# Attention and feed-forward block on one core: the projections of q, k, V and the output issued as four matmuls of 32 outputs each

## The chip, the cores and the metric

The kernel runs on one core of one Trainium2 chip. The metric is the device time of one execution in microseconds (us). Names of engines: PE is TensorE's matmul, PEld its weight load, ACT is ScalarE, DVE is VectorE, POOL is GpSimd, SP is SyncE. PSUM is the memory that matmuls write to, SBUF the one that everything else works in.

## What is computed

One transformer block on x of 4 batches x 1024 tokens x 256 features, all in float32:

```python
# attention, 16 heads of 16
xn = layernorm(x)
q, k, v = split(xn @ Wqkv.T)                 # 256 features each, 16 heads of 16
attn = softmax(q @ k.T / sqrt(16))           # per batch and head, 1024 x 1024
y = concat_heads(attn @ v) @ Wout.T
x = x + layernorm(y)
# feed-forward, 256 -> 1024 -> 1024 -> 1024 -> 256
xn = layernorm(x)
h = silu((xn @ w1.T) * s1) * ((xn @ w2.T) * s2)
h = gelu((h @ h1.T) * sh1)
h = gelu((h @ h2.T) * sh2)
x = x + layernorm((h @ w3.T) * s3)
```

## The kernel before

`tile_fast` does the work. (`tile_general` is a slower path for other inputs; it runs only when a flag says so, and the change doesn't touch it.) A first stage computes the attention of all four batches, a second one the feed-forward network of all tokens.

**The units of attention.** The 16 heads are taken in four groups of four. A unit is one batch, one group of heads and one half (512) of the queries: 4 x 4 x 2 = 32 units, each with 16 tiles. A tile is 128 keys x 512 queries for two heads. Its scores (`exponentials`, L451) are two matmuls that use 64 of the 128 rows of the array each and all 128 columns, side by side; ACT then takes the exponential of both in one instruction of 128 x 1024 (L452). Two tiles together hold the four heads of a group. The weighted sums (`weigh`, L459) are for each pair of tiles four matmuls, one for each head, which use all 128 rows and 32 columns of the array each and write to partitions 0 to 31, 32 to 63, 64 to 95 and 96 to 127 of one PSUM tile. A float32 matmul becomes two weight loads and two matmuls on the chip, so one call of `weigh` is eight matmul instructions in two rounds of four. A matmul of the float32r kind (scores, feed-forward) becomes one of each.

**The main loop** (L868 to L888) goes round five or six times for each unit. Once round makes the scores of three tiles (`TURN`; fewer where a step has borrowed a PSUM tile), weighs the tiles made the time before, two at a time, and then calls `side.take()`.

**The side steps.** `Side` holds lists of steps, and `take` runs those that are due, at most one of them with matmuls ("tensor" steps). So in PE's program order one such step stands between the weighted sums of one round and the scores of the next. These steps are the prologue of the next batch (layer norm, transposes of x, projections), and the end of each unit and each batch (division, transposes, output projection). Three of them are what the change touches:

- `project(w, m, h)` in `prologue`, L324: q (w = 0) or k (w = 1), 128 of the 256 features, 512 tokens. Two matmuls (over `c`, the halves of the 256 inputs) with 128 x 128 weights from `wqk_sb`, that read 128 x 512 of `xT`. 8 steps for each batch, 32 in all.
- `values(t0)` in `prologue`, L315: V of 256 tokens. Four matmuls whose weights are 128 x 128 of `xT`, that read 128 x 256 of `wv_sb`. 4 steps for each batch.
- `project(t0)` in `ending`, L516: the output projection of 256 tokens. Four matmuls whose weights are 128 x 128 of `oT`, that read 128 x 256 of `wo_sb`. 4 steps for each batch.

Each of these steps writes one PSUM tile from `ps_misc`, which has a single buffer; DVE copies it out (ACT in the first and the last steps). The first batch's projections for the first groups of heads run ahead of the loop (L836 to L849). The last half's output projection runs inside the feed-forward stage, whose matmuls (L697, L750) have 128 x 128 weights.

The transposes (L305, L478, L480, L506) are matmuls of 128 x 128 by an identity.

Of the kernel before, what the change touches and what calls it, by code (L numbers as in the profile page):

```python
# [18 lines left out]
P = 128  # L19
HEADS = 16  # L20
DH = 16
SLOT = 32
# [13 lines left out]
NQ = 512  # L36
# [4 lines left out]
@with_exitstack  # L41
def tile_attention_ffn_block(ctx: ExitStack, tc: tile.TileContext, x, wqk, wv, wo, w1, w1s, w2, w2s, h1, h1s, h2, h2s, w3, w3s, out):

    nc = tc.nc
    B, S, D = x.shape
    bad = ctx.enter_context(tc.tile_pool(name="flag", bufs=1)).tile([1, 1], I32, name="bad")
    tile_fast(tc, x, wqk, wv, wo, w1, w1s, w2, w2s, h1, h1s, h2, h2s, w3, w3s, out, bad)
    failed = nc.values_load(bad[0:1, 0:1], min_val=0, max_val=1 << 24)
    with tc.If(failed > 0):
        tile_general(tc, x, wqk, wv, wo, w1, w1s, w2, w2s, h1, h1s, h2, h2s, w3, w3s, out)
# [46 lines left out]
def tile_fast(ctx: ExitStack, tc: tile.TileContext, x, wqk, wv, wo, w1, w1s, w2, w2s, h1, h1s, h2, h2s, w3, w3s, out, bad):  # L115
    nc = tc.nc
    B, S, D = x.shape
    HID = w1.shape[1]
    DC = D // P
# [3 lines left out]
    HPT = P // DH  # L123
# [53 lines left out]
    with ExitStack() as actx, ExitStack() as rctx:  # L177
        aw = actx.enter_context(tc.tile_pool(name="aw", bufs=1, side="right"))

        wqk_sb = aw.tile([P, DC, 2, HEADS, DH], F32, name="wqk_sb")  # L180
        wv_sb = aw.tile([P, DC, D], F32, name="wv_sb")
        wo_sb = aw.tile([P, DC, D], F32, name="wo_sb")
# [51 lines left out]
        def misc(name):  # L234
            return ps_misc.tile([P, NQ], F32, tag="misc", name=name)

        def check_weights(n, c):
# [15 lines left out]
            def count(j):  # L253
                def run():
                    w, r = (t[:, NQ * j : NQ * (j + 1)] for t in (st["w"], st["r"]))
                    i = k * (WIDE // NQ) + j
                    nc.vector.scalar_tensor_tensor(w, w, 1.0, r.bitcast(F32), ALU.mult, ALU.not_equal, accum_out=misses[:, i : i + 1])
                    if NQ * (j + 1) == WIDE:
                        nc.gpsimd.dma_start(out=rows(rounded[n]).bitcast(F32), in_=st["r"].bitcast(F32).rearrange("p (i d) -> p i d", i=rows_at_once[n]))

                return run

            return [Step(load, 0, False), Step(cast, 3, False)] + [Step(count(j), 1, False) for j in range(WIDE // NQ)]

        def to_scalar(o, i, scale=1.0):
            nc.scalar.activation(o, i, AF.Copy, scale=scale)  # L266

# [3 lines left out]
        def prologue(b, space, copy):  # L271

            st = {}
# [36 lines left out]
            def values(t0):  # L310
                def run():
                    pv = space(f"pv_{b}_{t0}").rearrange("p (t d) -> p t d", d=D)
                    for i in range(2):
                        for c in range(DC):
                            nc.tensor.matmul(pv[:, i, :], st["xT"][:, c, (t0 + i) * P : (t0 + i + 1) * P], wv_sb[:, c, :], start=c == 0, stop=c == DC - 1)  # L315
                    copy(cv[:, t0 : t0 + 2, :], pv)

                return run

            def project(w, m, h):  # L320
                def run():
                    pp = space(f"p{w}_{b}_{m}_{h}")
                    for c in range(DC):
                        nc.tensor.matmul(pp, wqk_sb[:, c, w, HPT * m : HPT * (m + 1), :], st["xT"][:, c, h * NQ : (h + 1) * NQ], start=c == 0, stop=c == DC - 1)  # L324
                    hi, lo = (cq[w, m, k][:, h * NQ : (h + 1) * NQ] for k in ("hi", "lo"))
                    scale = 1.0 if w else 1.0 / math.sqrt(DH)
                    copy(hi, pp, scale)
                    nc.vector.scalar_tensor_tensor(lo, pp, scale, hi.bitcast(F32), ALU.mult, ALU.subtract)

                return run  # L330
# [11 lines left out]
            def total(m):  # L342
                def run():
                    if m == 0:
                        st["norm"] = work.tile([P, NT], F32, tag="norm", name=f"norm_{b}", bufs=1)
                        st["sum"] = work.tile([P, DC], F32, tag="sum", name="sum", bufs=1)
                        st["sum2"] = work.tile([P, DC], BF16, tag="sum2", name="sum2", bufs=1)
                    t = st["sum"][:, m : m + 1]
                    nc.vector.tensor_reduce(t, cq[1, m, "hi"].bitcast(F32), AX.X, ALU.add)
                    nc.gpsimd.tensor_tensor(st["sum2"][:, m : m + 1], t, t, ALU.mult)  # L350

                return run
# [46 lines left out]
            flags = [Step(total(m), 1, False) for m in range(DC)]  # L399
# [95 lines left out]
        def ending(b, h, copy):  # L495

            st = {}

            def transposes(c):
                def run():  # L500
                    if c == 0:
                        st["oT"] = work.tile([P, DC, NQ], F32, tag="oT", name=f"oT_{b}_{h}", bufs=1)
                        st["y"] = (both if h else work).tile([P, TPQ, D], F32, tag="y", name=f"y_{b}_{h}", bufs=1)
                    pt = misc(f"po_{b}_{h}_{c}")
                    for t in range(TPQ):
                        nc.tensor.transpose(pt[:, t * P : (t + 1) * P], on[h][:, t, c * P : (c + 1) * P], ident)  # L506
                    copy(st["oT"][:, c, :], pt)

                return run

            def project(t0):
                def run():
                    py = misc(f"py_{b}_{h}_{t0}").rearrange("p (t d) -> p t d", d=D)
                    for i in range(2):
                        for c in range(DC):
                            nc.tensor.matmul(py[:, i, :], st["oT"][:, c, (t0 + i) * P : (t0 + i + 1) * P], wo_sb[:, c, :], start=c == 0, stop=c == DC - 1)  # L516
                    copy(st["y"][:, t0 : t0 + 2, :], py)

                return run

            def gather(i):
                def run():
                    st["mv"] = norms.gather([st["y"][:, j, :] for j in range(i, i + 2)], i, st.get("mv"))

                return run

            def root():
                st["ln"] = norms.root(st["mv"])

            def apply(i0):  # L530
                def run():
                    for i in range(i0, i0 + 2):
                        norms.apply(st["y"][:, i, :], st["y"][:, i, :], st["ln"], i)

                return run

            def residual(i):
                def run():
                    xr = xs[b][:, h * TPQ + i : h * TPQ + i + 2, :]
                    nc.vector.tensor_add(xr, xr, st["y"][:, i : i + 2, :])  # L540

                return run

            return (
                [Step(transposes(c), 1) for c in range(DC)] + [Step(project(t), 1) for t in range(0, TPQ, 2)]
                + ([Step(open_ffn, 0, False)] if (b, h) == (B - 1, NH - 1) else [])
                + [Step(gather(i), 1, False) for i in range(0, TPQ, 2)] + [Step(root, 0, False)]
                + [Step(apply(i), 1, False) for i in range(0, TPQ, 2)] + [Step(residual(i), 1, False) for i in range(0, TPQ, 2)]
            )
# [253 lines left out]
        def feed_forward():  # L803

            chain = ends[B - 1, NH - 1]
            for n in range(len(halves_of)):

                gated(ffn["a"], 2 if n else 1)
                if n + 1 < len(halves_of):
                    chain[0].extend(prepare(n + 1, to_scalar))  # L810
                if n == 1:
                    side.add(judge())
                gelu_layer(ffn["b"], ffn["a"], "h1")
                gelu_layer(ffn["a"], ffn["b"], "h2")
                side.flush()
                chain = side.add(finish(n, ffn["a"]), True)
            side.flush()
# [10 lines left out]
        norm, xt, qk, v, flags = prologue(0, first_space, first_copy)  # L828
# [39 lines left out]
        while weighed < len(tiles):  # L868
# [7 lines left out]
            while weighed + 2 <= n:  # L876
                b, g, h, c, _ = tiles[weighed]
# [252 lines left out]
```

## Time and profile before

| | us |
|---|---|
| median of 3 runs (1335.29 to 1335.87) | 1335.56 |
| the profiled execution, its own time | 1335.65 |
| its span, first to last instruction | 1333.7 |
| PE busy | 1271.8 (95%) |
| PEld busy | 797.1 (60%) |
| DVE busy | 724.3 (54%) |
| ACT busy | 696.6 (52%) |
| POOL busy | 120.7 (9%) |

The span is the stretch of one profiled execution from its first to its last instruction; 1.95 us of the execution's own time lie around it. The granted clock of PE is 0.994 of full speed over the span. Attention takes the first 680 us or so and the feed-forward stage the rest.

A row of the timeline merges neighbouring instructions of one line: start in us, length in us, engine, line, operation, output<-inputs, array shape (rows*columns), operand, count, and in brackets the idle time before it with what ended it. The recorded end of a matmul is modelled and lies after the start of the next one, so the distance from start to start is what a matmul takes from PE; I read lengths of work that way.

### The profile page before, as it was taken

The numbers are of one execution on the slowest core, as the hardware profiler recorded it, in microseconds if no ns is written. First come the engines' busy times: TensorE is split into PE (matmuls) and PEld (weight loads), VectorE is DVE, ScalarE is ACT, GpSimd is POOL, SyncE is SP. The second block draws the span as 40 slices with busy tenths as digits, with TensorE's granted clock in tenths as the row PEclk, the third lists the DMA queues.
The fourth block names the chain that finished last, engine by engine and source line by source line (L and its number), as shares of the span: only waits on it lengthen the run. The fifth ranks groups of instructions, "written<-read, shape, count | busy, mean of one in ns | idle before, by whom it ended". The sixth has DMA issues, their size and how long they took to land.

```text
span 1333.7 us, 18779 instructions
## 1 busy us (share of the span) xinstructions
PE 1271.8 (95%) x7042; PEld 797.1 (60%) x7042; DVE 724.3 (54%) x1561; ACT 696.6 (52%) x847; POOL 120.7 (9%) x166
## 2 busy tenths in 40 slices
PE   7999999999999999989999999999999999999996
PEld 3334333343343434333478888888888888888885
DVE  3575669756696455645482553735436364362623
ACT  4587788877887787888741321414224141231410
POOL 6120112111111000000000000000000000000000
PEclk9999999999999999999999999999999999999998
DMA  4675344544444433235220000000000000000000
GB/s 133 152 194 111 98 97 113 122 111 99 120 106 106 77 64 62 45 64 179 79 111 1 1 16 1 17 0 0 16 1 16 0 16 2 0 17 0 17 0 19
DMA packets 38661, 79.61 MB, mean 60 GB/s; under 512 B 11296, under 2 KB 21152, under 8 KB 38560
## 3 DMA queue, kind: packets, MB, share of 16 engines
q1 hardware_dynamic: 30672, 53.66, 18.3%
q0 software_dynamic: 7360, 24.12, 5.5%
q8 instruction: 58, 0.95, 0.3%
q10 hardware_dynamic: 528, 0.52, 0.1%
q14 instruction: 43, 0.35, 0.1%
HBM read 28.98 MB, written 15.73 MB: 34 GB/s over the span
## 4 chain that ended last, share of the span: by engine, by line
PE 78%; DVE 9%; ACT 7%; issue 2%; POOL 1%; DMA 0%; SPq 0%; ACTq 0%; POOLq 0%; DVEq 0%
PE ph L697 35%; PE acc L459 13%; PE s L451 8%; ACT e L452 6%; PE pg L697 6%; PE pz L750 4%; PE p L324 4%; PE py L516 2%; PE pv L315 2%; DVE top L468 2%; PE po L480 1%; DVE o L269 1%; DVE sg L713 1%; DVE st L93 1%; DVE ha_lo L702 1%
## 5 line engine op out<-in xcount | busy, mean ns | idle before, releaser
L452 ACT ACTIVATE e<-s 128x1024 f32<-128x1024 f32 x512 | 486.3, 1036 | 131.1 <-PE s L451 117.8
L459 PE MATMUL acc<-e,vaug 128*32 128x512 f32 x2048 | 256.5, 603 | 2.9 <-POOL vaug L429 2.9
L733 ACT ACTIVATE a<-ph,h_scale 128x512 f32<-128x512 f32 x128 | 81.0, 685 | 306.9 <-PE ph L697 306.9
L451 PE MATMUL s<-sq,sk 64*128 64x512 f32 x1024 | 193.9, 449 | 24.7 <-ACT e L452 22.7
L697 PE MATMUL ph<-hb_lo,h 128*128 128x512 f32 x512 | 199.4, 389 | 0.0
L697 PE MATMUL ph<-hb_hi,h 128*128 128x512 f32 x512 | 199.4, 389 | 0.0
L451 PEld LDWEIGHTS s<-sq,sk 64*128 64x128 f32 x1024 | 86.3, 184 | 159.4 <-ACT e L452 124.5
L468 DVE TENSOR_TENSOR top<-top,e 128x512 f32<-128x512 f32 x192 | 134.1, 699 | 35.7 <-ACT e L452 30.1
L459 PEld LDWEIGHTS acc<-e,vaug 128*32 128x32 f32 x2048 | 49.4, 109 | 108.5 <-issue 98.1
L734 DVE CAST ha_hi<-a 128x512 fp32r<-128x512 f32 x64 | 27.1, 424 | 158.2 <-ACT a L733 158.2
L103 POOL TENSOR_TENSOR rstd<-ve,minus_half 128x4 f32<-128x4 f32 (+1 forms) x33 | 37.5, 1136 | 791.6 <-DVE ve L101 791.6
L697 PEld LDWEIGHTS ph<-hb_lo,h 128*128 128x128 f32 x512 | 96.1, 188 | 20.1
L697 PEld LDWEIGHTS ph<-hb_hi,h 128*128 128x128 f32 x512 | 96.1, 188 | 20.2
L697 PE MATMUL ph<-ha_hi,sq 128*128 128x512 f32 x256 | 101.9, 398 | 0.4
L697 PE MATMUL ph<-ha_lo,sq 128*128 128x512 f32 x256 | 99.8, 390 | 0.0
L697 PE MATMUL ph<-ha_lo,sk 128*128 128x512 f32 x256 | 99.7, 390 | 0.0
L697 PE MATMUL ph<-ha_hi,sk 128*128 128x512 f32 x256 | 99.7, 390 | 0.0
L713 DVE SCALAR_TENSOR_TENSOR sg<-pg,w_scale,sg 128x512 f32<-128x512 f32 x64 | 47.1, 745 | 47.7 <-ACT sg L711 47.7
L711 ACT ACTIVATE sg<-pg,w_scale 128x512 f32<-128x512 f32 x64 | 43.3, 688 | 56.6 <-DVE ha_lo L702 48.4
L734 DVE CAST hb_hi<-a 128x512 fp32r<-128x512 f32 x64 | 27.0, 422 | 82.2 <-ACT a L733 82.2
L324 PE MATMUL p<-xT,wqk_sb 128*128 128x512 f32 x128 | 64.0, 626 | 0.9 <-ACT xT L266 0.9
L697 PEld LDWEIGHTS ph<-ha_hi,sq 128*128 128x128 f32 x256 | 48.2, 188 | 12.7 <-DVE sg L713 3.4
(145 smaller groups left out, 1663.6 us busy)
## 6 DMA issues: line engine op xcount, KB each, us to landing
w<-in_h_dram POOLq DMA_DIRECT2D x16, 512.0 KB, 4.6
h_r<-wr POOLq DMA_DIRECT2D x16, 512.0 KB, 3.8
sk<-ck1hi SPq DMA_DIRECT2D x64, 64.0 KB, 2.3
sk<-ck1lo SPq DMA_DIRECT2D x64, 64.0 KB, 2.3
sq<-cq1hi SPq DMA_DIRECT2D x64, 64.0 KB, 2.3
sq<-cq1lo SPq DMA_DIRECT2D x64, 64.0 KB, 2.3
h<-h_r SPq DMA_DIRECT2D x8, 512.0 KB, 6.5
sk<-ck0hi SPq DMA_DIRECT2D x56, 64.0 KB, 2.3
```

The costliest lines, as they stand in the source:

```text
L103: nc.gpsimd.tensor_tensor(rstd[:, :n], ve[:, :n], self.minus_half[:, :n], ALU.pow)
L324: nc.tensor.matmul(pp, wqk_sb[:, c, w, HPT * m : HPT * (m + 1), :], st["xT"][:, c, h * NQ : (h + 1) * NQ], start=c == 0, stop=c == DC - 1)
L451: nc.tensor.matmul(s[:, a, :], stacks[1, g % 2, u][r, c * P : (c + 1) * P], stacks[0, g % 2, u][r, h * NQ : (h + 1) * NQ], start=True, sto ...
L452: nc.scalar.activation(pair(k)[:, u], s, AF.Exp)
L459: nc.tensor.matmul(acc[SLOT * i : SLOT * (i + 1), :], vaug[g % 2][:, c, i, :], pair(k)[:, i // 2, i % 2, :], start=c == 0, stop=c == NT - 1)
L468: nc.vector.tensor_max(top, top if c > 1 else pair(k - 2)[:, :, :, 0:P], pair(k)[:, :, :, 0:P])
L697: nc.tensor.matmul(p, homes[n][c][:, m * P : (m + 1) * P], half[:, c, :], start=c == 0 and k == 0, stop=c == len(homes[n]) - 1 and k == 1)
L711: nc.scalar.activation(sg, p[:, 0, :], AF.Silu, scale=scales["w1"][:, m : m + 1])
L713: nc.vector.scalar_tensor_tensor(sg, p[:, 1, :], scales["w2"][:, m : m + 1], sg, ALU.mult, ALU.mult)
L733: nc.scalar.activation(a, p[:, j, :], AF.Gelu, scale=scales[n][:, m : m + 1])
L734: nc.vector.tensor_copy(o[0][:, m, :], a)
L750: nc.tensor.matmul(p[t], half[:, c, t * P : (t + 1) * P], homes["w3"][c], start=c == 0 and k == 0, stop=c == HC - 1 and k == 1)
```

## The change

A helper `by_slots` takes the place of `nc.tensor.matmul` in the three steps. It issues, for one 128 x 128 set of weights, four matmuls with 32 of its columns each, which read the same moving operand and write 32 partitions each of the same PSUM tile. Nothing else is changed: the order of the steps, what they read and write, and their arithmetic are the same.

```diff
+        def by_slots(o, w, i, **flags):
+
+            for j in range(0, P, SLOT):
+                nc.tensor.matmul(o[j : j + SLOT, :], w[:, j : j + SLOT], i, **flags)
+
...
                     for i in range(2):
                         for c in range(DC):
-                            nc.tensor.matmul(pv[:, i, :], st["xT"][:, c, (t0 + i) * P : (t0 + i + 1) * P], wv_sb[:, c, :], start=c == 0, stop=c == DC - 1)
+                            by_slots(pv[:, i, :], st["xT"][:, c, (t0 + i) * P : (t0 + i + 1) * P], wv_sb[:, c, :], start=c == 0, stop=c == DC - 1)
...
                     for c in range(DC):
-                        nc.tensor.matmul(pp, wqk_sb[:, c, w, HPT * m : HPT * (m + 1), :], st["xT"][:, c, h * NQ : (h + 1) * NQ], start=c == 0, stop=c == DC - 1)
+                        heads = wqk_sb[:, c, w, HPT * m : HPT * (m + 1), :].rearrange("p h d -> p (h d)")
+                        by_slots(pp, heads, st["xT"][:, c, h * NQ : (h + 1) * NQ], start=c == 0, stop=c == DC - 1)
...
                     for i in range(2):
                         for c in range(DC):
-                            nc.tensor.matmul(py[:, i, :], st["oT"][:, c, (t0 + i) * P : (t0 + i + 1) * P], wo_sb[:, c, :], start=c == 0, stop=c == DC - 1)
+                            by_slots(py[:, i, :], st["oT"][:, c, (t0 + i) * P : (t0 + i + 1) * P], wo_sb[:, c, :], start=c == 0, stop=c == DC - 1)
```

## The prediction

> **What bounds the kernel now.** I read the page's busy shares first, then the groups of PE with shapes kept apart, then the timeline around one projection.
>
> ```profile
> PE 1271.8 (95%) x7042; PEld 797.1 (60%) x7042; DVE 724.3 (54%) x1561; ACT 696.6 (52%) x847; POOL 120.7 (9%) x166
> ...
> PE 78%; DVE 9%; ACT 7%; issue 2%; POOL 1%; DMA 0%; SPq 0%; ACTq 0%; POOLq 0%; DVEq 0%
> ```
>
> PE is busy 95% and has 78% of the chain. From 26 to 660 us, which is attention, a table by windows gives PE 593.3 busy and ACT 501.5. So PE leads there too, though ACT is near. The groups:
>
> ```profile
> L459 PE MATMUL acc<-e,vaug 128*32 128x512 f32 x2048 | 256.5, 603 | 2.9 <-POOL vaug L429 2.9
> ...
> L324 PE MATMUL p<-xT,wqk_sb 128*128 128x512 f32 x128 | 64.0, 626 | 0.9 <-ACT xT L266 0.9
> L315 PE MATMUL pv<-wv_sb,xT 128*128 128x256 f32 x128 | 31.8, 391 | 0.0
> L516 PE MATMUL py<-wo_sb,oT 128*128 128x256 f32 x128 | 31.7, 390 | 1.8 <-DVE oT L269 1.3 <-ACT oT L266 0.5
> ```
>
> L459 already has the shape that the change gives to the other three: 2048 instructions in 256.5 us are 0.50 us for four, as much as one of L324 (64.0 / 128 = 0.50). Four narrow matmuls side by side cost no more than one wide one. What differs is what lies between shapes. The timeline of PE around one projection, and below it one that weighs two pairs of tiles:
>
> ```profile
> 476.82 0.40 PE L451 MATMUL s<-sq,sk 64*128 64x512 f32 x2
> 477.15 1.06 PE L459 MATMUL acc<-e,vaug 128*32 128x512 f32 x8
> 478.14 1.98 PE L324 MATMUL p<-xT,wqk_sb 128*128 128x512 f32 x4
> 480.06 0.96 PE L451 MATMUL s<-sq,sk 64*128 64x512 f32 x6
> ...
> 484.08 1.92 PE L459 MATMUL acc<-e,vaug 128*32 128x512 f32 x16
> 485.94 0.50 PE L451 MATMUL s<-sq,sk 64*128 64x512 f32 x2
> ```
>
> From start to start, 8 narrow matmuls take 0.99 us and 16 take 1.86: a round of four costs 0.43 and the stay in the shape 0.13 more. The projection takes 1.92 for four matmuls. By the single starts in the trace its first is followed after 533 ns and the others after 429. The last narrow matmul before it is followed after 523, not 429. So the entry to the wide shape costs 94 ns, in which nothing streams, and 104 ns, in which the first 128-column load is not hidden. Into the narrow shape the load shows far less: the first round takes 453 ns in place of 429, 24 more.
>
> A step that already has the narrow shape, the head bound at L360, shows what no entry looks like:
>
> ```profile
> 552.47 1.93 PE L459 MATMUL acc<-e,vaug 128*32 128x512 f32 x16
> 554.22 0.40 PE L360 MATMUL pn<-sq,heads_bf 128*32 128x512 bf16 x4
> ```
>
> and its loads
>
> ```profile
> 553.36 0.13 PEld L459 LDWEIGHTS acc<-e,vaug 128*32 128x32 f32 x4 [0.30 <-issue]
> 553.79 0.12 PEld L360 LDWEIGHTS <-heads_bf 128*32 128x32 bf16 x4 [0.30 <-issue]
> ```
>
> Its four loads start 0.43 us ahead of its matmuls, during the last round of weighted sums. Its first matmul comes 409 ns after the last narrow one, which is 429 from round to round (a round's four starts are 20 ns apart). All four steps of this kind that follow weighted sums show 409. Neither the 94 nor any load is paid.
>
> [...]
>
> **The change part by part.** A projection of q or k goes from 4 matmuls and 4 loads to 16 and 16; so do 8 and 8 of V and of the output projection to 32 and 32. In all 384 of each become 1536. No DMA, no wait and no instruction on another queue is added or moved. A step's first load still carries the same wait for its PSUM tile, and only its last matmul releases DVE.
>
> *q and k after weighted sums.* Now, from the start of the last round: 541 (429 + 20 + 92 of drain) to the projection, then 533 + 429 + 429 + 523 = 1914 to the scores; sum 2455 ns. After: 429 for that round, 3 x 429 for three of the four new ones, 541 for the last; sum 2257. Gain 0.20 us.
>
> *V and output projection after weighted sums.* Now 541 + 1924 (320 first, 6 x 215, 309 to the scores) = 2465. After: 429 + 7 x 215 + (309 + 20) = 2263, if a round of four 256-column matmuls takes the 215 ns that one wide one takes now. Gain 0.20. A round's loads take 109 each and start 7 apart, 130 in all, inside 215.
>
> *How many.* Of the 64 steps, read off PE's order, 46 follow weighted sums directly: 22 of L324, 11 of L315, 13 of L516. Two L516 steps waited about 0.7 us for `oT`; [...]so they save the load alone (104 to 24, less 20 for the wider end: 0.06). So do ten that follow scores: they change shape on entry either way. Sum: 44 x 0.20 + 12 x 0.06 = 8.8 + 0.7 = 9.5 us.
>
> *What it costs.* Three L516 steps run inside the feed-forward stage:
>
> ```profile
> 660.04 0.40 PE L697 MATMUL pg<-cq0lo,cq1lo 128*128 128x512 f32 x1
> 660.28 1.89 PE L516 MATMUL py<-wo_sb,oT 128*128 128x256 f32 x8
> 661.82 0.58 PE L697 MATMUL pg<-cq0hi,ck0hi 128*128 128x512 f32 x1
> 662.24 0.39 PE L697 MATMUL pg<-cq0lo,ck0hi 128*128 128x512 f32 x1
> ```
>
> Same shape, and no gap on either side: 2.20 us from the first to the last start. After: entry 94 + 24, the round's 20, exit 94 and then an exposed load of 104, about 0.33 each; the one that waits for `oT` pays no entry, 0.14. Sum 0.8 us lost. The opening steps (12.7 to 25.6 us) wait for ACT's `xT` on entry and their followers for DVE or DMA: I take 0, bounds -0.3 and +0.5.
>
> *Does the gain reach the end?* It counts if PE is what the next scores wait for. In ACT's timeline over the same stretch the exponentials idle and are released by PE:
>
> ```profile
> 476.88 2.86 ACT L452 ACTIVATE e<-s 128x1024 f32<-128x1024 f32 x3 [1.85 <-PE s L451]
> 480.60 1.94 ACT L452 ACTIVATE e<-s 128x1024 f32<-128x1024 f32 x2 [0.86 <-PE s L451]
> ```
>
> ACT had done at 479.74, 0.32 us ahead of the scores at 480.06. That is the cover. Over the steps after weighted sums it is mostly 0.32 to 1.5 us, twice 0.22; both exceed 0.20. After every one of these steps the scores start without a wait. Then ACT also starts 0.20 earlier, and a later round in which ACT leads begins earlier by as much. DVE gets its tile earlier. If the cover were gone, what is late next is the exponential.
>
> Sum: 9.5 - 0.8 = 8.7 us. The profiled execution took 1335.65 us (span 1333.7 and 1.95 around it), 0.09 above the median of 1335.56. 1335.65 - 8.7 = **1327.0 us**.
>
> **What the trace doesn't show.** (a) Rounds with 256 columns: 8 instructions in 215 ns, 27 ns each. The densest stretch of 1.7 us now has 36 instructions, 47 ns each. [...] From above, 47 ns each would give 376. I take 215: PE's sequencer starts two waits back to back 106 ns apart and 126 apart where a load and a matmul stand between (as at 24.99 and 25.10 us), so these two take it 20 ns, and eight take 80. (b) Four groups that read one moving operand; L459 and L360 read four different ones. A loss would come if these reads collide, and two at a time would double a round, 384 rounds by at least 0.2, 77 us or more[...]. I take none. (c) More instruction fetch: 2304 more on PE's 14,084, and none of today's idle time is put down to fetch. I take 0.
>
> **The rivals.**
> 1. *The sequencer sets the pace of 256-column rounds* (slower). There are 256 of them. At 47 ns an instruction: 256 x 0.161 = 41 us lost, 1335.65 - 8.7 + 41 = 1368. It decides from 31 ns an instruction on, where 256 x (8 x 31 - 215) ns = 8.5 us eats the gain. For it: no longer stretch so dense in the trace. Against: the 20 ns above, and loads and matmuls 2 to 5 ns apart at the start of a round. With (b): 0.14.
> 2. *ACT takes over.* The cover of 0.32 us is near 0.20. If half of the 44 steps lose their gain to the next exponential: 1327.0 + 4.4 = 1331.4. For: ACT idles only 115.8 us before exponentials released by PE in attention. Against: no wait after these steps now. 0.08.
> 3. *The narrow step drains all the same*, since the first load's wait or the new moving operand stops the prefetch. Then only loads change: 56 x 0.06 - 0.8 = 2.6 gained, 1333.1. Against: L360, whose first load comes from another tile too. 0.05.
>
> **How the numbers follow.** Forecast as worked out: 0.73, its own range 1325.5 to 1329.0 by the bounds of the opening and the cover. Rivals 2 and 3 take it to 1334, 0.13 more; these and the forecast are 0.86, and the slow rival is left outside. A measurement can tell about 0.2%, 2.7 us, from no change. Faster: 0.73 + 0.08 = 0.81; same: rival 3, which lies at that edge, 0.05; slower 0.14. Range 1324.8 to 1334.0.
>
> **What would show it.** Right: L324, L315 and L516 with shape 128*32 and 512 instructions each; starts 409 ns from the last weighted sum to the step; four rounds at 429 or eight at 215; an idle PE no larger before L451. Wrong: rounds of V above 250 ns (rival 1), scores after a step that wait for ACT (rival 2), 523 ns ahead of the step (rival 3).

## The result, and the profile after

The changed kernel takes 1328.56 us (median of 5 runs, 1328.08 to 1330.6) against 1335.56 before: 7.0 us less, a ratio of 0.9946 with a 95% interval of 0.9935 to 0.9958. The profiled execution took 1328.08, its span is 1326.3. On another chip the same pair gave 0.994 (0.9927 to 0.9952), 1328.34 against 1335.98. The forecast was 8.7 us less, 1327.0. Here and below an interval is that of the ratio over all runs, and "us less" after a ratio is the ratio's share of the time before. The medians can differ by another amount, since the runs of one kernel spread over 2 to 6 us.

In the changed kernel a line number after the helper is 5 or 6 higher, and all matmuls of the three steps carry the helper's line, L268. Its page first:

```profile
PE 1264.8 (95%) x8194; PEld 777.2 (59%) x8194; DVE 723.2 (55%) x1561; ACT 697.0 (53%) x847; POOL 120.5 (9%) x166
```

PE has 1152 matmuls more and 7.0 us less of busy time; DVE, ACT and POOL have the same work. PE's groups with shapes kept apart:

```profile
L465 PE MATMUL acc<-e,vaug 128*32 128x512 f32 x2048 | 255.1, 600 | 1.4 <-POOL vaug L435 1.4
...
L268 PE MATMUL p<-xT,wqk_sb 128*32 128x512 f32 x512 | 62.3, 608 | 0.9 <-ACT xT L271 0.9
L268 PE MATMUL pv<-wv_sb,xT 128*32 128x256 f32 x512 | 32.1, 393 | 0.0
...
L268 PE MATMUL py<-wo_sb,oT 128*32 128x256 f32 x512 | 30.7, 380 | 1.7 <-DVE oT L274 1.3 <-ACT oT L271 0.5
```

Four times the instructions in about the same busy time (125.1 us in all, 127.5 before). The timeline of PE around one of the projections in the loop, then its weight loads:

```profile
470.09 1.06 PE L465 MATMUL acc<-e,vaug 128*32 128x512 f32 x8
470.97 1.90 PE L268 MATMUL p<-xT,wqk_sb 128*32 128x512 f32 x16
472.80 0.96 PE L457 MATMUL s<-sq,sk 64*128 64x512 f32 x6
```

```profile
470.09 0.16 PEld L465 LDWEIGHTS acc<-e,vaug 128*32 128x32 f32 x8 [0.36 <-issue]
470.87 0.23 PEld L268 LDWEIGHTS p<-xT,wqk_sb 128*32 128x32 f32 x8 [0.62 <-PE s L457]
```

Sums, projection and scores took 2.91 us from the first sum to the first score before (477.15 to 480.06); here they take 2.71. The projection's first loads stand at 470.87, 0.10 ahead of its matmuls and inside the last round of sums (0.43 ahead in 32 of the 46 steps that follow sums); they no longer wait for the sums to end. A step of V and one in the feed-forward stage:

```profile
126.75 1.91 PE L268 MATMUL pv<-wv_sb,xT 128*32 128x256 f32 x32
128.59 0.96 PE L457 MATMUL s<-sq,sk 64*128 64x512 f32 x6
```

```profile
651.94 0.39 PE L703 MATMUL pg<-cq0lo,cq1lo 128*128 128x512 f32 x1
652.26 1.93 PE L268 MATMUL py<-wo_sb,oT 128*32 128x256 f32 x32
654.12 0.50 PE L703 MATMUL pg<-cq0hi,ck0hi 128*128 128x512 f32 x1
654.46 0.40 PE L703 MATMUL pg<-cq0lo,ck0hi 128*128 128x512 f32 x1
```

V's 32 matmuls take 1.84 to the scores. In the feed-forward stage, from the first row to the last, it is 2.52 us, where it was 2.20. PE's longest wait in attention, from the table of waits (us in all, times, longest), and below it the same row before:

```profile
PE s L457 <- ACT e L458: 22.6, 62, 0.7
```

```profile
PE s L451 <- ACT e L452: 22.7, 62, 0.7
```

The shorter steps brought no wait for the exponential. What the forecast didn't have is in the opening, here of the changed kernel and then of the kernel before:

```profile
13.18 5.33 PE L268 MATMUL p<-xT,wqk_sb 128*32 128x512 f32 x32
18.70 1.64 PE L310 MATMUL pt<-ident,xn 128*128 128x128 f32 x8 [0.19 <-DVE xn L111]
21.28 3.64 PE L268 MATMUL p<-xT,wqk_sb 128*32 128x512 f32 x32 [0.94 <-ACT xT L271]
24.74 1.91 PE L268 MATMUL pv<-wv_sb,xT 128*32 128x256 f32 x32
27.64 0.70 PE L457 MATMUL s<-sq,sk 64*128 64x512 f32 x2 [0.99 <-DMA sq<-cq0hi]
```

```profile
12.68 4.80 PE L324 MATMUL p<-xT,wqk_sb 128*128 128x512 f32 x8
...
23.76 1.89 PE L315 MATMUL pv<-wv_sb,xT 128*128 128x256 f32 x8
25.58 0.51 PE L451 MATMUL s<-sq,sk 64*128 64x512 f32 x2
```

The first scores start at 27.64, against 25.58 before, and they wait 0.99 us for a copy by DMA.

### The profile page after: what moved, and what is told of

Its sections match the earlier page's. It is cut to its first block, busy times and chain, and to the rows that moved or that the text cites. A ratio compares the mean times of both kernels' runs of the same rounds, so it can differ in the third digit from the quotient of the medians.

```text
span 1326.3 us, 21103 instructions
## 1 busy us (share of the span) xinstructions
PE 1264.8 (95%) x8194; PEld 777.2 (59%) x8194; DVE 723.2 (55%) x1561; ACT 697.0 (53%) x847; POOL 120.5 (9%) x166
## 4 chain that ended last, share of the span: by engine, by line
PE 75%; DVE 12%; ACT 8%; issue 2%; DMA 1%; SPq 1%; ACTq 0%; POOL 0%; POOLq 0%; DVEq 0%
PE ph L703 35%; PE acc L465 12%; PE s L457 8%; ACT e L458 7%; PE pz L756 4%; PE p L268 4%; PE pg L703 4%; PE py L268 2%; DVE top L474 2%; PE pv L268 2%; DVE sg L719 2%; PE po L486 1%; DVE ha_lo L708 1%; DVE o L274 1%; DVE st L93 1%
## 5 line engine op out<-in xcount | busy, mean ns | idle before, releaser
L457 PE MATMUL s<-sq,sk 64*128 64x512 f32 x1024 | 194.0, 449 | 25.5 <-ACT e L458 22.6
L268 PE MATMUL p<-xT,wqk_sb 128*32 128x512 f32 x512 | 62.3, 608 | 0.9 <-ACT xT L271 0.9
```

The costliest lines, as they stand in the source:

```text
L268: nc.tensor.matmul(o[j : j + SLOT, :], w[:, j : j + SLOT], i, **flags)
L457: nc.tensor.matmul(s[:, a, :], stacks[1, g % 2, u][r, c * P : (c + 1) * P], stacks[0, g % 2, u][r, h * NQ : (h + 1) * NQ], start=True, sto ...
```

## The experiments

Theory A holds the opening's 2.06 us for chance (where a stretch of half clock falls, when a DMA lands). Theory B holds it for an effect of the narrow groups. A stretch of half clock is one in which the profile shows the clock granted to PE at 0.5 of full speed; a round of four matmuls then takes 855 ns in place of 429 (as from 14.04 to 14.89 us of the changed kernel). The time after "against" is that of the kernel before, measured on the same chip.

**Narrow in the loop only**

```diff
+        narrow = [False]
         def by_slots(o, w, i, **flags):
+            if not narrow[0]:
+                nc.tensor.matmul(o, w, i, **flags)
+                return
...
         alone = False
+        narrow[0] = True
...
         def feed_forward():
+            narrow[0] = False
```

> Narrow groups only in the steps inside the attention loop; the opening steps (before the loop) and the three output projections inside the feed-forward stage are issued as before, 128 wide. In the trace of the changed kernel the loop gained 10.0 us from its first scores to the first feed-forward matmuls, the opening lost 2.06 us and the feed-forward stage 0.6. Theory A (the opening lost by chance: where a stretch of half clock fell and when a DMA landed): only the 0.6 comes back, about 0.5 us faster than the changed kernel, 1328.0. Theory B (narrow groups themselves make the opening slower): 2.06 + 0.6 come back, 1325.9. Both: L268 steps inside the loop as in the changed kernel, 409 ns after the last weighted sum; the three steps in the feed-forward stage again without gaps.

Measured 1329.31 (1326.65 to 1330.95) against 1335.83; ratio 0.9944 (0.993 to 0.9957), 7.5 us less. The loop's steps are as in the changed kernel and the first scores start at 25.48, without a wait for DMA. The runs spread over 4 us, so the time can't separate 1328.0 from 1325.9.

**Narrow in the opening only** (the same switch, True, then False)

> The reverse: narrow groups in the opening steps alone (four projections of q and k and the first step of V), all else as before the change. Theory A: within 0.3 us of the time before, 1335.6, first scores between 25.3 and 27.6 us with the half clock wherever it falls. Theory B: 2 us slower, 1337.6, first scores at 27 us or later.

Measured 1336.18 (1335.6 to 1338.34) against 1335.83; ratio 1.0001 (0.9993 to 1.0009), which is -0.9 to +1.2 us and leaves no room for B's 2. Yet in the profile the first scores start at 26.27, 2.63 us after V's first matmul in place of 1.82: a wait of 0.8 us, as in the changed kernel. That is what is left of B, too small for the time to show. (The stages after the opening stay 0.6 us late in this profile, but that figure is a balance: a half-clock stretch at 28.2 us cost 1.6 more by 50 us, and the kernel before lost 1.6 to its own at 59.3.) A fetch packet falls at 21.4 to 23.6 us here too (*A fetch moved forward*, below); that it makes the wait is not shown.

**Two groups of 64** (in `by_slots`: `range(0, P, 2 * SLOT)` and `j + 2 * SLOT`)

> The same three kinds of steps in two groups of 64 outputs in place of four of 32: narrow too, but not the shape of the weighted sums. Theory 1 (what is saved is the change of shape, with its drain): 523 ns from the last weighted sum to the step remain, only the first load shrinks from 104 ns exposed to about 50; 56 steps x 0.05 = 2.8 us less the feed-forward stage's 0.7: 1333.5. Rival (any narrow load is hidden and any column group overlaps what came before): 409 to 430 ns to the step, near 1328.6 as with groups of 32.

Measured 1335.81 (1332.61 to 1337.91) against 1335.83; ratio 0.9994 (0.9984 to 1.0003), 0.8 us less (-0.4 to 2.1). PE's timeline and loads at a projection:

```profile
474.75 1.04 PE L465 MATMUL acc<-e,vaug 128*32 128x512 f32 x8
475.73 1.94 PE L268 MATMUL p<-xT,wqk_sb 128*64 128x512 f32 x8
477.59 0.96 PE L457 MATMUL s<-sq,sk 64*128 64x512 f32 x6
```

```profile
475.72 0.20 PEld L268 LDWEIGHTS p<-xT,wqk_sb 128*64 128x64 f32 x4 [0.84 <-issue]
476.21 0.14 PEld L268 LDWEIGHTS p<-xT,wqk_sb 128*64 128x64 f32 x2 [0.29 <-issue]
```

The first loads come with the step (475.72, 475.73), not during the sums. By single starts every one of these steps that didn't wait for its input stands 522 to 523 ns after the last sum, and the first round is 50 ns longer than the next (480 and 429): theory 1 to the number. Two groups of 64 keep the 523 ns; four of 32, the shape of the sums beside them, take 409. The steps in groups of 64 save 56 x 0.047 = 2.6, less 0.8 in the feed-forward stage: 1.8 us, inside the interval of the time.

**q and k only, and V and output only** (`nc.tensor.matmul` kept in the other calls)

> Only the projections of q and k in groups of 32; V and the output projection 128 wide as before. By the forecast's sums: 22 steps after weighted sums x 0.198 + 6 after scores x 0.06 = 4.7 us, nothing lost in the feed-forward stage; 1335.56 - 4.7 = 1330.9, less what the opening costs (0 by theory A, up to 2 by theory B: 1332.9).

Measured 1333.36 (1330.0 to 1335.47) against 1335.83; ratio 0.9972 (0.9961 to 0.9982), 3.7 us less (2.4 to 5.2). The 4.7 of the sums is inside, the 2.7 of theory B too. In the profile the q and k steps that follow sums start 409 to 410 ns after the last sum (one that waits for its PSUM tile 491), those of V and the output 522 to 523: each kind goes by its own shape.

> Only V and the output projection in groups of 32; q and k 128 wide. By the forecast's sums 22 steps after weighted sums x 0.20 + 2 that waited and 4 after scores x 0.06 = 4.8 us, less 0.6 in the feed-forward stage: 4.2 us. With q and k alone (2.5 us measured, 4.7 forecast) the two should add up to what the whole change gives.

Measured 1334.53 (1331.63 to 1336.73) against 1335.98; ratio 0.9986 (0.9979 to 0.9993), 1.9 us less (0.9 to 2.8), short of 4.2. In its profile, between the same scores of both kernels, the stretch from 74 to 635 us is 4.0 us shorter than before, where its steps should save 19 x 0.198 + 5 x 0.06 = 4.1; but by 50 us it has fallen 1.2 us behind, and a half-clock stretch lies at 32.8 us. The two parts add up to 5.6, within what their intervals and the whole's 7 to 8 allow. The shortfall of this one goes with a lower granted clock over its 21 runs (*Clock*, below).

**More warm-up** (`WARM = 8` in place of 4; the third also has the switch of the first experiment)

> The kernel before with 8 warm-up matmuls in place of 4 (L834), nothing else: they end near 10 us, just ahead of the first transposes at 10.5, so that no idle stretch lies before the opening. In the profiles so far the opening's projections fall into one or two half-clock stretches of 3.4 us. Theory A (the part of the gain that is missing went into half-clock stretches that fall by chance): the opening runs at full clock, first scores near 24 us in place of 25.6, about 1.3 us faster than before, and the times of the runs lie closer together. Rival (the opening is paced by ACT and the DMA of the weights, the clock doesn't matter): no change.

> The changed kernel with the same 8 warm-up matmuls. Theory A: the distance to the kernel before with 8 is what the steps save, 9.96 in the loop less 0.6 in the feed-forward stage, 9 us, plus or minus chance stretches later on: near 1325.5. Theory B (narrow groups themselves slow the opening down by 2 us): the distance stays 7 us, first scores 1 us or more later than in the kernel before with 8.

> Narrow groups in the attention loop only, 128 wide in the opening and in the feed-forward stage, and 8 warm-up matmuls: the version that the runs point to. 0.6 us faster than the changed kernel with 8 warm-up matmuls by theory A (the three steps in the feed-forward stage), 2.6 by theory B.

Measured 1334.88, 1327.34 and 1327.18 against 1337.26 of the kernel before; ratios 0.9983 (0.9974 to 0.9991), 0.9931 (0.9917 to 0.9944) and 0.9923 (0.9909 to 0.9938). The opening's projections ran at full clock in all three (3.64 to 3.70 us for two). The change is worth 1334.88 - 1327.34 = 7.5 us there, between the two theories. With twice the warm-up the kernel before gains 2.4 us, of which only 0.6 is seen in its first scores (25.02); all of it goes with a higher granted clock (0.9948 on average, 0.9928 with 4). Its runs lie 3.0 us apart and those of the kernel before on that chip 3.2; so warm-up didn't make the times steadier, and A's forecast of that failed. The narrow opening (second kernel) still waits:

```profile
22.71 1.91 PE L268 MATMUL pv<-wv_sb,xT 128*32 128x256 f32 x32
26.02 0.70 PE L457 MATMUL s<-sq,sk 64*128 64x512 f32 x2 [1.40 <-DMA sq<-cq0hi]
```

1.40 us, behind steps that ran at full clock (3.64 us for the last two projections, 1.91 for V), so the clock isn't that wait's cause. With the wide opening (third) the first scores start at 24.48, without it. These two are the fastest kernels run, 1.5 us apart in that place and not to be told apart in time; nor do their ratios clear the changed kernel's own intervals.

**Rounds of 128 columns** (V and output)

```diff
-                        for c in range(DC):
-                            by_slots(pv[:, i, :], ..., wv_sb[:, c, :], ...)
+                        for n in range(0, D, P):
+                            for c in range(DC):
+                                by_slots(pv[:, i, n : n + P], ..., wv_sb[:, c, n : n + P], ...)
```

> The changed kernel with the rounds of V and of the output projection cut in two: 128 columns of the moving operand each, 16 rounds a step, 64 loads and 64 matmuls. It measures how near the sequencer is to being the bound. By the 20 ns for a load and a matmul (80 for a round) the stream of 107 ns or the loads of 109 to 130 ns set the round: 107 to 130 ns, a step 1.7 to 2.1 us. Rival (47 ns an instruction, the densest stretch before the change): 376 ns a round, a step 6 us and the kernel 130 us slower.

One run, 1328.45 us, so the answer is the profile's and not the time's. PE's timeline at one step of V:

```profile
126.68 1.93 PE L268 MATMUL pv<-wv_sb,xT 128*32 128x128 f32 x64
128.54 0.96 PE L458 MATMUL s<-sq,sk 64*128 64x512 f32 x6
```

64 loads and 64 matmuls in 1.86 us, rounds of 109 ns by single starts: 8 instructions in 109 ns, 13.6 each. (The expectation's 107 was an estimate, half of the 215 of a 256-column round.) The rival of 47 ns an instruction is out.

**A fetch moved forward**

```diff
             nc.tensor.matmul(idle, zeros[:, 0:P], zeros, start=True, stop=True)
+        for _ in range(36):
+            nc.tensor.matmul(idle[0:1, 0:1], zeros[:, 0:1], zeros[:, 0:1], start=True, stop=True)
```

> The kernel before (128 wide everywhere) with 36 matmuls of one row and one column after the warm-up ones, 144 instructions on PE more, as many as the narrow groups add to the opening; PE has nothing else to do there (6.8 to 10.5 us). In the four profiles whose opening issues V's first step in groups of 32 a 16 KB packet of instruction fetch falls at 21.5 to 23.5 us, among the copies that the first scores wait for, and from V's first matmul to the first scores it is 2.5 to 3.3 us; in the six others the packet falls at 28 us or later and it is 1.8 to 1.9. Theory C (the fetch delays those copies): here too the packet falls near 22 us and the first scores wait for a DMA, 2.5 us or more after V's first matmul, with wide matmuls. Rival (narrow matmuls themselves delay them): the packet falls early and the scores start 1.8 us after V as in the kernel before.

Measured 1335.45 (1333.78 to 1338.15) against 1335.98; ratio 0.9994 (0.9985 to 1.0003). A fetch packet here is one of the queue that the page calls "q8 instruction": 58 packets and 0.95 MB in the kernel before, 16 KB each. The first fell at 13.05 us, ahead of all the copies, and the first scores started 1.82 us after V. That separates nothing: the packet has to fall among the copies for the test. What supports theory C is a look at SP's queue. SP issues one copy of 32 KB in about 0.6 us (0.51 to 0.63 in most). In the changed kernel, and below it in the kernel before:

```profile
22.27 0.53 SPq L419 DMA_DIRECT2D sq<-cq0hi  x1
22.90 2.18 SPq L419 DMA_DIRECT2D sq<-cq0lo  x2
25.14 0.58 SPq L419 DMA_DIRECT2D sq<-cq0hi  x1
```

```profile
21.22 0.53 SPq L413 DMA_DIRECT2D sq<-cq0hi  x1
21.85 1.17 SPq L413 DMA_DIRECT2D sq<-cq0lo  x2
23.07 0.58 SPq L413 DMA_DIRECT2D sq<-cq0hi  x1
```

Two issues take 2.18 in place of 1.17. The second of the two runs from 23.49 to 25.08, and the table of DMA for 23.3 to 25 us of the changed kernel has one instruction packet, which the trace puts at 23.51 to 24.71:

```profile
q8 instruction: 1, 0.02, 4.4%
```

No other issue on SP there from 10 to 40 us takes over 0.81. In the kernel before, the first packet (36.11 to 37.27) lies over an issue of 1.34 us (36.10 to 37.44), the only one from 10 to 40 us over 0.72: so a held-up issue goes with the packet without narrow matmuls too. With 8 warm-up matmuls the changed kernel has two issues in 2.55 us from 20.87, and one packet between 21 and 23.5; in the second profile of the changed kernel two take 2.00 from 21.96. Over the whole span SP issues under 29 packets of the changed kernel, and under 24 of them one issue takes 1.1 to 2.0 us; in the kernel before it is 16 of 21, 1.1 to 1.8. Long issues come without it too: 10 and 8 of over 1 us lie under no such packet.

Where the packet falls at 21.4 to 23.6 (the changed kernel twice, opening only, 8 warm-ups, rounds of 128) the first scores start 2.5 to 3.3 us after V; where it falls elsewhere, 1.8 to 1.9, whether the opening is wide, narrow for q and k, narrow for V or in groups of 64. But the five profiles with late first scores are also just those whose opening has q, k and V all in groups of 32, with 144 instructions more on PE by the first scores. (The experiment's 144 ahead of the opening moved the packet of the kernel before from 36.11 to 13.05.) So that the late scores come from the packet is not shown: a narrow opening with the packet elsewhere wasn't tried.

**The step ahead of the third scores**

```diff
-            make(n + TURN)
             if weighed < len(tiles):
                 side.take()
+            make(n + TURN)
```

> Narrow groups in the loop only, and the side step taken ahead of the third tile's scores in the rounds where a step has borrowed a PSUM tile, in place of after them. The ten steps that followed scores then follow weighted sums, and two short stays in the shape of the scores become one. Theory 1 (each change of shape on PE costs 0.1 us of drain and a first load that shows): about 0.2 us saved in each of some 30 rounds, up to 6 us less than with narrow groups in the loop only, 1323. Rival (ACT has too little work queued in these rounds): the third exponential starts up to 2 us later and ACT sets the pace there, 1330 or more.

Measured 1337.8 (1334.52 to 1339.7) against 1335.98; ratio 1.0006 (0.9996 to 1.0015), some 8 us above narrow groups in the loop only by the two ratios. The rival holds. The table of waits:

```profile
PE s L462 <- ACT e L463: 36.2, 79, 0.7
```

36.2 us in 79 waits, against 22.6 in 62. The 13.6 us more of waiting outweigh what fewer changes of shape can save (up to 6 by the expectation): a change of shape less was worth nothing here, where the step that moves up keeps work from ACT.

**The changed kernel again**

> The changed kernel again, beside the others on the same chip and with a second profile: 7 to 8 us below the kernel before; in the profile the loop's steps as before (409 ns after weighted sums, 2.24 us to the scores), a fetch packet among the copies of the opening, first scores 2.5 us or more after V's first matmul; the half-clock stretches elsewhere than in its first profile if they fall by chance.

Measured 1328.34 (1327.86 to 1329.64); ratio 0.994 (0.9927 to 0.9952), 8.0 us less. The packet fell at 22.56, the first scores at 26.51, 2.72 after V. In its second profile the half clock fell elsewhere too. Around 403 us, where PE has waited three times for ACT (the second profile, then the first):

```profile
402.71 0.49 PE L457 MATMUL s<-sq,sk 64*128 64x512 f32 x2 [0.41 <-ACT e L458]
403.13 3.17 PE L465 MATMUL acc<-e,vaug 128*32 128x512 f32 x16
```

```profile
402.85 0.50 PE L457 MATMUL s<-sq,sk 64*128 64x512 f32 x2 [0.42 <-ACT e L458]
403.29 1.92 PE L465 MATMUL acc<-e,vaug 128*32 128x512 f32 x16
```

The same 16 matmuls take 3.17 and 1.92; the mean clock from 404 to 408 us is 0.61 in the second profile and 1.00 in the first, though both have the same three waits of 0.34 to 0.42. The first profile has its one half-clock stretch between 25 and 600 us at 30.30 to 33.71, behind waits of 0.99 and 0.82 us for DMA, and the kernel before its one at 59.31 to 62.73, behind a wait of 2.20 us for `top`. So each of the three was seen behind waits of PE; that the waits bring it is not shown.

## Why the prediction was right

*Entry.* Right to the number. In all 44 steps that follow sums and don't wait for `oT`, the step starts 409 to 410 ns after the last sum, save one that takes 490: at 106.55 us it waited for its PSUM tile, which DVE frees when `cq0lo` is done (106.41), the one place where an earlier step met a later DVE. A step of q or k with its round of sums costs 2239 ns in place of 2437 (523 + 1914), one of V or the output 2249 in place of 2447: 0.198 each. After scores it is 2282 in place of 2343: 0.06. Groups of 64, with 522 to 523 ns and 0.047 us a step, show that it is the shape. (The prediction's 541 is 543 in the trace and its 215 is 216; both stand on either side of the difference and cancel.)

*256-column rounds.* 216 ns; the choice of 215 over 376 was right, with room to spare (13.6 ns an instruction in the rounds of 128). Four groups that read one operand cost nothing: a round takes what the one wide matmul took, 429 and 216.

*Cover.* ACT didn't take over (rival 2): 22.6 us of waits for it, 22.7 before. L360 was the right witness against rival 3: the step starts after 409 ns and not after 523.

*Feed-forward stage.* 2.52 - 2.20 = 0.32 for a full step, forecast 0.33; 0.8 in all, as forecast.

*Size.* The forecast of 8.7 lies at the end of the first interval (5.6 to 8.7 us) and inside the second (6.4 to 9.8): right, but on the high side. Two terms stood at nothing. One is the opening, taken as 0 with a bound of +0.5, under which "more instruction fetch" stood at 0. In the first profile it is 2.06 us. 0.50 of that is there when the first projection starts: the weights of q landed 0.46 later, at 9.78 for 9.32 us. (In all profiles they are copied between 9.0 and 10.9 us, mostly later where q and k are narrow in the opening; whether the change has a hand in that is open.) Then the first four rounds of that projection ran at half clock, for 6.8 us in place of 3.4: some 0.6. In the table of windows the third number from the end is PE's clock, first in the changed kernel and then before:

```profile
10.00:15.00 5.00, 4.04 (x20) 1.99 (x24) 3.55 (x13) 1.59 (x3) 0.71 (x1) 0.50 0.17 52
```

```profile
10.00:15.00 5.00, 4.50 (x11) 2.50 (x12) 3.55 (x13) 1.19 (x2) 1.01 (x1) 0.66 0.19 52
```

The wait for the copies is 0.99, and one of 0.6 us or more comes back in every profile with the whole opening narrow. The loop gained 9.96 us up to 638 us where its steps save 9.2. The 0.7 more is a balance of things that the two profiles don't share: the wait for `vaug` is 1.4 us in place of 2.9, and the half-clock stretch of the loop lies at 30.3 in place of 59.3 us. So the profile reads 9.4 from the steps and 0.7, less 0.8 and 2.06: 7.2, against 7.4 between the spans.

*Clock.* The other term at nothing is the granted clock. Its mean over each run is on record. On the second chip the 43 runs of the kernel before take 1334.38 us on average at 0.995 (9 runs), 1335.55 at 0.994 (13), 1337.24 at 0.993 (12) and 1338.23 at 0.992 (9): 1.3 us for each 0.001. The table compares each kernel with the kernel before on its chip, by the ratio and then at equal clock, which means against a straight line through the times of the kernel before over their clock. The clocks are rounded to 0.001, and the figures at equal clock are good to some 0.5 us, less so with 8 warm-ups, where the line (0.992 to 0.994) is carried beyond its runs.

| us less | by the ratio | at equal clock | by the sums of the steps |
|---|---|---|---|
| q and k only | 3.7 | 4.2 | 4.7 |
| V and output only | 1.9 | 4.3 | 4.2 |
| two groups of 64 | 0.8 | 1.4 | 1.8 |
| narrow in the loop only | 7.5 | 9.5 | 9.5 |
| the same, 8 warm-ups | 10.3 | 8.5 | 9.5 |
| the changed kernel again | 8.0 | 9.8 | 8.7 |
| the same, 8 warm-ups | 9.2 | 8.6 | 8.7 |
| narrow in the opening only | -0.1 | 0.4 | 0 |
| the kernel before, 8 warm-ups | 2.3 | -0.1 | 0 |
| the kernel before, a fetch moved | 0.8 | 0.1 | 0 |

At equal clock the sums hold to about 1 us. What is missing by the ratio goes with the clock, and not by chance alone: V and output only has 0.9919 on average over 21 runs, the kernel before beside it 0.9935 over 43, a difference of more than five standard errors; the loop only (6 runs) and the changed kernel again (5) lie 0.0017 and 0.0015 under theirs. Why narrow groups in the loop go with a lower mean clock is not shown, nor what the late scores of the opening cost in the time.

*Rival 1* is out by a factor of two: PE takes an instruction every 13.6 ns (rounds of 128) where a step of 256-column rounds needs one every 27.

## What to carry to other kernels

Where small steps of one array shape stand between matmuls of another, look at the start-to-start distances on both sides: here 94 ns more than from round to round, and the part of the first load that showed (104 ns for 128 columns, 24 for 32) were paid at a change of shape. The steps here could be issued in their neighbour's shape at no cost of their own (429 and 216 ns a round, as before), but they gained only beside that neighbour (0.20 us a step), and lost where the shapes had agreed before (0.32 us a step in the feed-forward stage). Count the instructions that this adds in a stretch where critical DMAs are being issued: under 24 of 29 fetch packets of the changed kernel an issue on SP took 1.1 to 2.0 us in place of 0.6. And compare runs at the same granted clock before a small shortfall is explained: 0.001 of it was worth 1.3 us here, and a gain of 4.3 read as 1.9.

## What the runs showed of the hardware that was not expected

- A 16 KB fetch packet on q8, 0.9 to 1.6 us long in both kernels, mostly goes with a held-up DMA issue on SP: one of 1.1 to 2.0 us in place of 0.6 under 24 of the 29 packets of the changed kernel under which SP issues. With 2304 instructions more on PE, q8 has 9 packets more (67 for 58).
- PE took 64 loads and 64 matmuls in 1.86 us in the rounds of 128, at 109 ns a round 27 ns for a load and a matmul; in the changed kernel the starts of a round's four groups are 7 ns apart.
- The loads of a group of 64 columns show 50 ns at a change of shape (groups of 64), of 32 columns 24, of 128 columns 104 (both in the kernel before).
- The clock granted to PE was 0.5 of full speed for 3.41 us from 59.31 in the kernel before and from 30.30 in the changed kernel, behind waits of PE of 2.20 us and of 0.99 and 0.82. Around 403 us three waits of 0.34 to 0.42 had such a stretch behind them in one profile of the changed kernel and none in the other; it cost 1.25 us over 16 matmuls of the sums.
- A run's mean granted clock goes with its time: 1.3 us for each 0.001 over 43 runs of the kernel before.
